# Routed experts of a two-layer decoder: the gated product turned by DRAM and VectorE instead of TensorE

## The chip, the cores and the metric

One core of one Trainium2 chip runs the whole program. The time is the device time of one execution in microseconds; the kernel before takes 2071.18 us (median of three runs, 2070.22 to 2071.78). A profile is one execution recorded by the hardware profiler; line numbers such as L1244 are lines of the kernel before.

TensorE (PE) multiplies, and a row PEld is its loading of weights; VectorE is DVE in the profile, ScalarE is ACT, GpSimd is POOL and SyncE is SP. SP, ACT and POOL can issue DMAs. A DMA issued by SP or ACT goes to a hardware queue (q1 in the profile is SP's, q10 is ACT's), one issued by POOL to the software queue q0.

## The reference

Two decoder layers work on x of 16 blocks x 128 tokens x 512, each with self-attention, cross-attention and a feed-forward part, a layer norm after each of the six parts. Only the last part, the mixture of experts, is touched by the change:

```python
logits = x @ gate_weight.T                      # E = 8 experts
topk_w, topk_idx = top_k(softmax(logits), 2)    # combine[t, e] = weight of a chosen expert, else 0
gu  = einsum('th,efh->tef', x, gate_up_weights) # F = 352, gate and up
act = silu(gu[..., :F]) * gu[..., F:]
y   = einsum('tef,te,ehf->th', act, combine, down_weights)
sgu = x @ shared_gate_up.T                      # a shared expert, Fs = 704
y   = y + (silu(sgu[:, :Fs]) * sgu[:, Fs:]) @ shared_down.T
x   = layernorm(x + y)
```

All values are float32.

## The kernel before

Five stages come first: first attention, second attention, the ternary feed-forward part, and the two attentions of the second layer. They are the same in both kernels. The last stage computes the router, sorts each (token, choice) pair into a slot of its expert, and writes the token's row into `slots_x` in DRAM, with its weight and its destination in two columns ahead of it (`told`). Each expert's slots are padded to whole tiles of 128 rows, so there are NT = 39 tiles at most. Meanwhile PE computes the shared expert's hidden values (`hidden`, L1116), and keeps its down products (`po`, L1299 and L1307) as small tasks that are dealt out between the tiles.

The loop over the 39 tiles is a pipeline of steps. A `Tile` has these parts:

- `load` (L1214): POOL gathers the expert's weights, `ew`, 128 rows of 4352 floats, by an indirect DMA. Three buffers are held. Where a buffer already holds the right expert, the index is out of bounds and nothing is moved.
- `fetch` (L1226, L1228): SP loads the tile's rows from `slots_x` in four parts of 64 KB (`xs`), in an order in which VectorE's transpose of 32 x 32 squares completes the turn of the whole tile, and `told`.
- `turn` (L1233): that transpose on VectorE, 128 x 512, from `xs` to `xsT`.
- `up` (L1244): on PE the gate product `rg` and the up product `ru`, four matmuls each (a float32 matmul is two passes in the profile, so eight rows each); Silu on ScalarE (L1249); the product `ract` on VectorE (L1251).
- `turn_act` (L1256 to L1259): three PE transposes of `ract` against the identity into PSUM (`rt`), and two VectorE copies into `ractT`.
- `down` (L1265): three matmuls into `ry`. When they are done POOL may issue the weights of the tile after the next but one (`following.load()`, the same buffer). VectorE scales the result by the routing weight (L1276), and POOL adds it into `sums` in DRAM by an indirect DMA (L1277).

In step s the code calls `turn_act` of tile s-2, `turn` of s, `up` of s-1, `down` of s-2, and then deals one share of `po`. A planner orders the instructions of each engine, except those under `keep_in_program_order`, which stay as written. The order on PE after the first tiles is: `rt` of tile t-1, `rg` and `ru` of t, `ry` of t-1, some `po`; so `ry` of a tile stands behind `rg` and `ru` of the next tile.

The same kind of turn by way of DRAM is used elsewhere in the kernel: in the second stage `sq` is stored to `away` (L628) and read back in four loads as `pT` (L631), and `Turn` (L145, L151) does it for x.

Of the kernel before, what the change touches and what calls it, by code (L numbers as in the profile page):

```python
# [12 lines left out]
F32 = mybir.dt.float32  # L13
F32R = mybir.dt.float32r
AF = mybir.ActivationFunctionType
ALU = mybir.AluOpType
AX = mybir.AxisListType

P = 128
# [14 lines left out]
FE = 352  # L34
NX = E + 2
FS = 2 * FE
ECH = (128, 128, 96)
# [3 lines left out]
NT = 2 * NB + E - 1  # L41
# [5 lines left out]
def decoder_kernel(ctx: ExitStack, tc: tile.TileContext, a: dict, out: bass.AP):  # L47
    nc = tc.nc
# [4 lines left out]
    dram = ctx.enter_context(tc.tile_pool(name="dram", bufs=1, space=bass.MemoryType.DRAM))  # L53
# [19 lines left out]
    def bank(tag, shape, name):  # L73
        return psum.pool.tile(shape, F32, tag=tag, name=name, bufs=psum.banks[tag])
# [4 lines left out]
    ident = const.tile([P, P], F32, tag="ident", name="ident")  # L79
# [52 lines left out]
    QP = P // 4  # L132
# [206 lines left out]
    with tc.tile_pool(name="p1", bufs=1) as p1:  # L339
# [10 lines left out]
        with tc.tile_pool(name="p1a", bufs=1, side="right") as p1a:  # L350
# [5 lines left out]
            w = p1a.tile([P, KC, 640], F32, tag="w", name="w")  # L356
# [340 lines left out]
    with tc.tile_pool(name="p3", bufs=1) as p3:  # L697
# [34 lines left out]
        for g in range(NG):  # L732
# [4 lines left out]
            for f in range(NF0):  # L737
# [4 lines left out]
                for dst, wt in ((pa, w1), (pb, w2)):  # L742
                    for k in range(KC):
                        for n in range(2):
                            nc.tensor.matmul(  # L745
                                dst, lhsT=wt[:, k, f * P : (f + 1) * P], rhs=xs[n][:, k, :],
                                start=(k == 0 and n == 0), stop=(k == KC - 1 and n == 1),
                            )
                sg = p3.tile([P, TG], F32, tag="sg", name="sg", bufs=2)
# [11 lines left out]
            else:  # L761

                for n in range(2):
                    t = pre.tile([P, 2, 3 * D], F32, tag="pre", name=f"wq4{n}")
# [168 lines left out]
    QP = P // 4  # L933
# [93 lines left out]
    with tc.tile_pool(name="p6", bufs=1, reuse_waits="tile") as p6:  # L1027
        acts, halves = {}, {}
# [8 lines left out]
        def gate_up(w):  # L1037
            return w[:, 0:GU].rearrange("p (k f) -> p k f", k=KC)
# [10 lines left out]
        with tc.tile_pool(name="p6a", bufs=1, side="right", reuse_waits="tile") as p6a:  # L1049
# [14 lines left out]
            tr = bank("mm", [P, GB, P], "tr")  # L1064
# [7 lines left out]
            def gt(name, shape=(P, NB, E)):  # L1072
                return p6a.tile(list(shape), F32, tag=name, name=name)


            lg, sc, top, eq = (gt(n) for n in ("lg", "gsc", "top", "eq"))
            m = gt("gm", (P, NB))
# [123 lines left out]
        with tc.tile_pool(name="p6r", bufs=1, side="right", reuse_waits="tile") as p6r:  # L1201
# [3 lines left out]
            class Tile:  # L1205
# [32 lines left out]
                def up(self):  # L1238
                    gu = gate_up(self.w)
                    pg = bank("sc", [P, FE], "rg")  # L1240
                    pu = bank("sc", [P, FE], "ru")
                    for dst, off in ((pg, 0), (pu, FE)):
                        for k in range(KC):
                            nc.tensor.matmul(  # L1244
                                dst, lhsT=self.xT[:, k, :], rhs=gu[:, k, off : off + FE],
                                start=(k == 0), stop=(k == KC - 1),
                            )
                    sg = p6.tile([P, FE], F32, tag="sg", name="rsg", bufs=3)
                    nc.scalar.activation(sg, pg, AF.Silu)  # L1249
                    self.act = p6r.tile([P, FE], F32, tag="ract", name="ract", bufs=2)  # L1250
                    nc.vector.tensor_tensor(self.act, sg, pu, ALU.mult)  # L1251

                def turn_act(self):
                    tr = bank("pt", [P, 3, P], "rt")
                    for m_, mw in enumerate(ECH):
                        nc.tensor.transpose(tr[:mw, m_, :], self.act[:, m_ * P : m_ * P + mw], ident)  # L1256
                    self.actT = p6r.tile([P, 3, P], F32, tag="ractT", name="ractT", bufs=2)
                    nc.vector.tensor_copy(self.actT[:, 0:2, :], tr[:, 0:2, :])
                    nc.vector.tensor_copy(self.actT[: ECH[2], 2, :], tr[: ECH[2], 2, :])  # L1259

                def down(self, following):
                    dn = down_w(self.w)
# [56 lines left out]
            ahead = {}  # L1319
# [15 lines left out]
            for step in range(NT + 2):  # L1335
                if 3 <= step + 2 < NT:
                    ahead[step + 2] = Tile(step + 2)
                    ahead[step + 2].fetch()
                if 0 <= step - 2:
                    ahead[step - 2].turn_act()  # L1340
                if step < NT:
                    ahead[step].turn()
                if 0 <= step - 1 < NT:
                    ahead[step - 1].up()
                if 0 <= step - 2:
                    ahead.pop(step - 2).down(ahead[step + 1] if step + 1 < NT else None)
                if step < NT:
                    share.deal()
# [188 lines left out]
```

## Time and profile before

| what | value |
|---|---|
| median of the runs | 2071.18 us |
| profiled execution, its own time | 2073.39 us |
| its span, first to last instruction | 2071.6 us |
| PE busy in the span | 2014.1 us, 97% |
| VectorE, ScalarE, POOL busy | 878.6, 627.6, 646.8 us |
| routed-expert tiles, first `rg` to about the last `ry` | 1667 to 2021 us |
| of these 354 us: PE, VectorE, ScalarE, POOL busy | 343.6, 104.6, 18.1, 97.5 us |
| DMA engines busy in these 354 us | 69% (software queue 57.0%, SP's queue 11.7%) |
| mean granted TensorE clock | 0.992 of full speed |

A row of groups gives the line, the engine, the operation, what is written from what, the shape and the count; then the busy time and the mean length of one in ns; then the idle time of the engine just before, and what ended it. A row of the timeline gives start and length in us, then the same names, and in brackets the idle time before. A row of a DMA queue gives packets, MB, and the time of its packets as a share of 16 engines over the window. Releasers are inferred from semaphore events, and the lengths of matmuls overlap.

### The profile page before, as it was taken

What the parts mean: (1) busy time and instruction counts of PE and PEld (TensorE: products, weight loads), DVE (VectorE), ACT (ScalarE), POOL (GpSimd) and SP (SyncE); (2) the same over time, 40 slices, a digit from 0 to 9 for tenths busy, and PEclk for the clock granted to TensorE, in tenths of its full rate; (3) what the DMA queues carried; (4) which work ended last, traced back from release to release, by engine and by line L of the source; (5) the groups of instructions that cost most, each with busy time, mean ns of one, the idle gap of its engine ahead of it and who ended that gap; (6) DMA issues with size and microseconds to landing.
All of it is one profiled execution on the core that took longest, in us unless ns stands there. A gap on an engine that the chain in (4) does not pass through costs nothing.

```text
span 2071.6 us, 25330 instructions
## 1 busy us (share of the span) xinstructions
PE 2014.1 (97%) x9093; PEld 1115.7 (54%) x9093; DVE 878.6 (42%) x1763; ACT 627.6 (30%) x2107; POOL 646.8 (31%) x674
## 2 busy tenths in 40 slices
PE   8999999999999999999999999999899999999997
PEld 4555554444444458888554445555544455555552
DVE  4777732444554254432134314777731122232234
ACT  3555532333333333222310112766622200000002
POOL 6445530111211113233322113455613222223223
PEclk9999989999999999999999999999999999999999
DMA  9201231344432232001310018500023256786844
GB/s 249 78 25 40 104 124 52 104 127 137 132 117 83 66 118 71 21 11 54 143 51 22 11 34 266 204 22 21 27 66 118 87 141 178 226 237 188 247 108 168
DMA packets 155470, 221.58 MB, mean 107 GB/s; under 512 B 49616, under 2 KB 110416, under 8 KB 150608
## 3 DMA queue, kind: packets, MB, share of 16 engines
q1 hardware_dynamic: 140448, 146.51, 22.6%
q0 software_dynamic: 13792, 72.14, 11.6%
q8 instruction: 72, 1.18, 0.2%
q10 hardware_dynamic: 1104, 1.31, 0.2%
q14 instruction: 54, 0.44, 0.1%
HBM read 182.73 MB, written 72.69 MB: 123 GB/s over the span
## 4 chain that ended last, share of the span: by engine, by line
PE 85%; DMA 5%; DVE 4%; POOL 3%; ACT 2%; issue 1%; SPq 0%; POOLq 0%; DVEq 0%; ACTq 0%
PE po L649 10%; PE po L176 7%; PE pq L590 5%; PE pq L841 5%; PE pq L165 5%; PE pg L1116 4%; PE ry L1265 4%; PE po L772 4%; PE pa L745 4%; PE pb L745 4%; DMA ew<-in_l1f_w_dram,which 4%; PE rg L1244 4%; PE ru L1244 4%; PE pu L1116 3%; PE pv L851 3%; PE av L637 3%
## 5 line engine op out<-in xcount | busy, mean ns | idle before, releaser
L226 POOL TENSOR_TENSOR p<-p,rs 128x512 f32<-128x512 f32 x192 | 200.0, 1043 | 504.0 <-DVE rs L225 494.7
L649 PE MATMUL po<-mT,cc 128*128 128x512 f32 x512 | 231.5, 600 | 0.2 <-ACT cc L642 0.2
L219 ACT ACTIVATE p<-t,nmx 128x128 f32<-128x128 f32 x512 | 198.6, 390 | 34.0 <-POOL p L226 10.2
L649 PEld LDWEIGHTS po<-mT,cc 128*128 128x128 f32 x512 | 95.1, 190 | 114.3 <-issue 106.3
L219 ACT ACTIVATE p<-sc,nmx 128x128 f32<-128x128 f32 x256 | 90.2, 374 | 117.8 <-DVE nmx L214 110.4
L590 PE MATMUL pq<-xT,wqr 128*128 128x512 f32 x256 | 115.7, 593 | 2.9 <-ACT xT L129 2.9
L1214 POOL DMA_INDIRECT ew<-in_l1f_w_dram,which x39 | 40.6, 1042 | 249.1 <-PE ry L1265 182.8
L176 PE MATMUL po<-wo,oT 128*128 128x512 f32 x256 | 116.9, 600 | 0.4 <-ACT qkT L454 0.4
L1249 ACT ACTIVATE rsg<-rg 128x352 f32<-128x352 f32 x39 | 18.1, 464 | 326.4 <-PE rg L1244 310.1
L115 POOL TENSOR_SCALAR ve<-mv 128x1 f32<-128x1 f32 x80 | 18.1, 226 | 303.0 <-DVE mv L113 289.1
L1244 PE MATMUL rg<-ew,xsT 128*128 128x352 f32 x312 | 101.8, 469 | 10.4 <-DMA ew<-in_l1f_w_dram,which 9.6
L841 PE MATMUL pq<-xT,wq 128*128 128x512 f32 x256 | 110.6, 592 | 0.7 <-ACT xT L129 0.7
L1265 PE MATMUL ry<-ew,ractT 128*128 128x512 f32 (+1 forms) x234 | 106.9, 592 | 0.0
L122 POOL TENSOR_SCALAR x<-x,mv,rstd 128x512 f32<-128x512 f32 x48 | 100.5, 2094 | 4.5
L1244 PE MATMUL ru<-ew,xsT 128*128 128x352 f32 x312 | 98.7, 459 | 0.0
L219 ACT ACTIVATION_READ_ACCUMULATOR p<-t,nmx 128x1 f32 x512 | 96.1, 188 | 0.0
L233 DVE COPY pT<-pt 128x512 f32<-128x512 f32 x128 | 86.6, 679 | 19.4 <-PE pt L231 19.4
L756 POOL TENSOR_TENSOR hl<-ht,hh 128x512 fp32r<-128x512 f32 x44 | 57.4, 1306 | 108.2 <-ACT hh L754 108.2
L231 PEld LDWEIGHTS pt<-ident,p 128*128 128x128 f32 x512 | 60.0, 141 | 55.7 <-issue 41.5
L1116 PE MATMUL pg<-xT,sw_gu 128*128 128x512 f32 x192 | 86.5, 593 | 0.0
L1277 POOL DMA_INDIRECT sums<-ry,place x39 | 61.8, 1585 | 74.7 <-DMA sums<-ry,place 37.8
L1251 DVE TENSOR_TENSOR ract<-rsg,ru 128x352 f32<-128x352 f32 x39 | 20.3, 521 | 151.0 <-issue 140.4
(243 smaller groups left out, 3676.4 us busy)
## 6 DMA issues: line engine op xcount, KB each, us to landing
piece<-in_l0f_w_dram SPq DMA_DIRECT2D x48, 352.0 KB
away<-sq SPq DMA_DIRECT2D x32, 512.0 KB
pT<-away SPq DMA_DIRECT2D x128, 128.0 KB
raw<-in_l0x_raw_dram SPq DMA_DIRECT2D x8, 1728.0 KB
slots_x<-zero SPq DMA_DIRECT2D x1, 10023.0 KB
sums<-zero SPq DMA_DIRECT2D x1, 9984.0 KB
xs<-slots_x SPq DMA_DIRECT2D x156, 64.0 KB
x<-turned SPq DMA_DIRECT2D x128, 64.0 KB
```

The lines of the kernel that those rows point to most:

```text
L122: engine.tensor_scalar(x[b], x[b], mean, rstd, ALU.subtract, ALU.mult)
L165: nc.tensor.matmul(got["p"], lhsT=lhsT, rhs=rhs, start=(n == 0), stop=(n == len(pairs) - 1))
L176: nc.tensor.matmul(po, lhsT=oT[:, c, :], rhs=wo[:, c, :], start=(c == 0), stop=(c == KC - 1))
L219: nc.scalar.activation(self.p[:, j, :], src[:, j, :], AF.Exp, bias=nmx[:, j : j + 1], accum_out=self.sm[:, j : j + 1])
L226: nc.gpsimd.tensor_tensor(self.p, self.p, spread(rs, P), ALU.mult)
L590: nc.tensor.matmul(pq, lhsT=wqr[:, k, cols], rhs=xT[:, k, :], start=(k == 0), stop=(k == KC - 1))
L649: nc.tensor.matmul(self.po, lhsT=self.cc[:, 4 * par + j, :], rhs=mT[h], start=(par == 0 and j == 0), stop=(par == 1 and j == 3),)
L745: nc.tensor.matmul(dst, lhsT=wt[:, k, f * P : (f + 1) * P], rhs=xs[n][:, k, :], start=(k == 0 and n == 0), stop=(k == KC - 1 and n == 1),)
L841: nc.tensor.matmul(pq, lhsT=wq4[k // 2][:, k % 2, c * P : (c + 1) * P], rhs=xT[:, k, :], start=(k == 0), stop=(k == KC - 1))
L1116: nc.tensor.matmul(dst, lhsT=sw_gu[:, k, at : at + P], rhs=xTs[g][:, k, :], start=(k == 0), stop=(k == KC - 1),)
L1244: nc.tensor.matmul(dst, lhsT=self.xT[:, k, :], rhs=gu[:, k, off : off + FE], start=(k == 0), stop=(k == KC - 1),)
L1265: nc.tensor.matmul(po, lhsT=self.actT[:mw, m_, :], rhs=dn[:mw, m_, :], start=(m_ == 0), stop=(m_ == 2))
```

## The change

The gated product no longer goes through PE to be turned. The multiply on VectorE is split in two and writes `act` with its columns in the order (fourth, chunk, 32) instead of (chunk, fourth, 32). ScalarE's queue stores it to `acts` in DRAM (three buffers), and four loads, two on ScalarE's queue and two on SP's, bring it back with each fourth of the columns on its own 32 partitions. Each load waits for the store. Two VectorE transposes of 32 x 32 squares then write `ractT`. The up product's PSUM bank and the Silu tile are widened to 384 columns so that they can be viewed in fourths. In a step, `turn` of tile s is called ahead of `turn_act` of tile s-2. `down` is the same, and so is all other code.

```diff
                 def up(self):
...
-                    sg = p6.tile([P, FE], F32, tag="sg", name="rsg", bufs=3)
-                    nc.scalar.activation(sg, pg, AF.Silu)
-                    self.act = p6r.tile([P, FE], F32, tag="ract", name="ract", bufs=2)
-                    nc.vector.tensor_tensor(self.act, sg, pu, ALU.mult)
+                    sg = p6.tile([P, 3 * P], F32, tag="sg", name="rsg", bufs=3)
+                    nc.scalar.activation(sg[:, 0:FE], pg, AF.Silu)
+                    act = p6r.tile([P, FE], F32, tag="ract", name="ract", bufs=2)
+                    def fourths(t):
+                        return t.rearrange("p (m q a) -> p m q a", m=3, a=QP)
+                    for q, to in (
+                        (slice(0, 3), act[:, 0 : 9 * QP].rearrange("p (q m a) -> p m q a", q=3, m=3)),
+                        (slice(3, 4), act[:, 9 * QP :].rearrange("p (m q a) -> p m q a", m=2, q=1)),
+                    ):
+                        n = to.shape[1]
+                        tc.keep_in_program_order(nc.vector.tensor_tensor(
+                            to, fourths(sg)[:, 0:n, q], fourths(pu)[:, 0:n, q], ALU.mult
+                        ))
+                    self.away = dram.tile([P, FE], F32, tag="acts", name="acts", bufs=3)
+                    nc.scalar.dma_start(self.away, act)
+                    self.act = p6r.tile([P, 4, 3 * QP], F32, tag="ract4", name="ract4", bufs=2)
+                    for q in range(4):
+                        w = (3 if q < 3 else 2) * QP
+                        (nc.scalar, nc.sync)[q % 2].dma_start(
+                            self.act[q * QP : (q + 1) * QP, :, 0:w],
+                            self.away.rearrange("(t r) f -> r t f", r=QP)[:, :, 3 * q * QP : 3 * q * QP + w],
+                        )
 
                 def turn_act(self):
-                    tr = bank("pt", [P, 3, P], "rt")
-                    for m_, mw in enumerate(ECH):
-                        nc.tensor.transpose(tr[:mw, m_, :], self.act[:, m_ * P : m_ * P + mw], ident)
                     self.actT = p6r.tile([P, 3, P], F32, tag="ractT", name="ractT", bufs=2)
-                    nc.vector.tensor_copy(self.actT[:, 0:2, :], tr[:, 0:2, :])
-                    nc.vector.tensor_copy(self.actT[: ECH[2], 2, :], tr[: ECH[2], 2, :])
+                    to = self.actT.rearrange("p m (t r) -> p t m r", r=QP)
+                    act = self.act.rearrange("p t (m a) -> p t m a", a=QP)
+                    for rows, ms in ((P, slice(0, 2)), (ECH[2], slice(2, 3))):
+                        tc.keep_in_program_order(nc.vector.transpose(to[:rows, :, ms], act[:rows, :, ms]))
...
+                if step < NT:
+                    ahead[step].turn()
                 if 0 <= step - 2:
                     ahead[step - 2].turn_act()
-                if step < NT:
-                    ahead[step].turn()
```

## The prediction

> **What bounds the kernel now.** I read the busy shares first, then the groups of the routed-expert stage, then its order in time, and last the DMA queues in short windows. The page's first part has TensorE (PE) busy for 97% of the 2071.6 us span. The changed code runs from the first `rg` matmul to the last `ry`, about 1667 to 2021 us. Groups of that stage (busy us, mean ns of one | idle before):
>
> ```profile
> L1265 PE MATMUL ry<-ew,ractT 128*128 128x512 f32 (+1 forms) x234 | 106.9, 592 | 0.0
> L1244 PE MATMUL rg<-ew,xsT 128*128 128x352 f32 x312 | 101.8, 469 | 10.4 <-DMA ew<-in_l1f_w_dram,which 9.6 <-issue 0.8
> L1244 PE MATMUL ru<-ew,xsT 128*128 128x352 f32 x312 | 98.7, 459 | 0.0
> L1256 PE MATMUL rt<-ident,ract 128*128 128x128 f32 (+1 forms) x117 | 19.3, 274 | 0.0
> ```
>
> The means overstate PE, since matmuls overlap; starts in time do not. Here is one step (start, length in us):
>
> ```profile
> 1748.65 0.52 DVE L1251 TENSOR_TENSOR ract<-rsg,ru 128x352 f32<-128x352 f32 x1 [2.85 <-issue]
> 1751.40 1.03 POOL L1214 DMA_INDIRECT ew<-in_l1f_w_dram,which  x1 [5.92 <-PE ry L1265]
> 1751.83 0.49 PE L1256 MATMUL rt<-ident,ract 128*128 128x128 f32 x3
> 1751.95 0.34 SPq L1228 DMA_DIRECT2D told<-slots_x  x1
> 1752.16 2.53 PE L1244 MATMUL rg<-ew,xsT 128*128 128x352 f32 x8
> 1753.62 2.13 SPq L1226 DMA_DIRECT2D xs<-slots_x  x4
> 1756.89 2.74 PE L1265 MATMUL ry<-ew,ractT 128*128 128x512 f32 x6
> 1757.15 0.52 DVE L1251 TENSOR_TENSOR ract<-rsg,ru 128x352 f32<-128x352 f32 x1 [3.56 <-issue]
> 1759.90 1.04 POOL L1214 DMA_INDIRECT ew<-in_l1f_w_dram,which  x1 [5.57 <-PE ry L1265]
> ```
>
> A step is 8.50 us (1748.65 to 1757.15): rg and ru 4.73, ry 2.58, about two shared `po` passes 0.86, transposes 0.33 (1751.83 to 1752.16). The chain that ended last leaves PE in this stage for one thing only, the weights:
>
> ```profile
> 1759.90 11.73 DMA ew<-in_l1f_w_dram,which
> 1771.67 2.63 PE rg L1244 x8
> ```
>
> A gather really moves weights only when the slot's expert changes. The software queue's bytes per step show it: after the first tiles there are seven runs of three consecutive real gathers (2.2 to 2.7 MB in each such step, 0.3 MB in the others). Their waits cost PE 12.9 us: the weight-load row (PEld `rg`) shows that sum in 11 waits, and the 9.6 of the matmul row are the same waits seen again.
>
> The last view decides this case: the queues while a weight gather flies (1753.4 to 1758.6 us; packets, MB, share of 16 engines). SP's four `xs` loads were issued at 1753.62.
>
> ```profile
> q0 software_dynamic: 101, 1.76, 84.4%
> q1 hardware_dynamic: 18, 0.01, 0.7%
> ```
>
> In 5.2 us the hardware queue moved 18 packets. In 1673 to 1675 us, just behind another gather, it moved 862:
>
> ```profile
> q1 hardware_dynamic: 862, 0.39, 97.4%
> ```
>
> So loads on SP's queue nearly stand still until the gather is through, and an `xs` issued at 1753.6 drains by about 1762. Nobody notices today: `xs` is fetched two steps ahead.
>
> **The change part by part.**
>
> *Transposes leave PE.* 39 tiles x 0.33 us = 12.9 us, the whole possible gain. In a step ended by a weight wait it is worth nothing, since the gather's landing doesn't move.
>
> *VectorE.* The multiply becomes two, of 288 and 64 columns. The 352-column row takes 521 ns and the 512-column copy from PSUM 687, so about 1 ns a column over a fixed 160: 0.45 + 0.22, about 0.65 us together, 0.15 more. Two PSUM copies (0.42 + 0.28) become two square transposes; 512 columns take 697 ns (`xsT`), so 256 and 96 rows of 128 take about 0.43 + 0.30. Even. VectorE is busy 105 of 354 us here: hidden, except on the way of `act` below. `turn` now stands ahead of `turn_act`, so `xsT` isn't held up by it. Queued behind a late `turn_act` on VectorE are the next tile's multiply, `place` and the scaling of `ry`.
>
> *DMA issues.* Per tile one store and two loads on ScalarE's queue, two loads on SP's ahead of later `xs` and `told`. A store takes 0.34 us to issue and a load 0.43 (SP rows of the `away`/`pT` pair in the second stage). ScalarE is busy 18 of 354 us, so 1.2 us a tile are free; but its next Silu stands behind the two loads, which wait for the store. SP gains 0.86 to its 2.1 us of a step: hidden. That ScalarE has a queue of its own helps no further by the Trainium skill (same page as below, section "Issuing engines are not separate DMA queues"): all queues end in the same 16 engines and only issue time is saved; no trace here shows the two queues under load yet, so the new traffic is costed as if on SP's.
>
> *DMA time.* Sixteen 64 KB loads used 20.2% of 18 us of all engines (1104 to 1122 us), 0.91 us for four of 512 packets. The new four have 512 smaller packets: 0.6 (by bytes) to 0.9 (by packets). The store at the rate of the final 256 KB `sum` loads (0.75 us each) is 0.5. Together 1.1 to 1.4 us a tile; without the cover of the idle DMA (31% of the stage) it would delay gathers by just that.
>
> *The round trip, on the path.* Let m be the start of the multiply. Store issued at m+0.65; a dependent load after a 256 KB store could start 2.08 us after its issue (1017.97 to 1020.05), here about 1.9; second load of each queue 0.45 later; its landing about 2.1 (the 256 KB `sum` took 2.62). Landed m+5.1, turned m+5.8. `ry` needs it at 1756.89 less the 0.33: m+7.9. So 2.1 us of slack, covered by ry, po, rg and ru of other tiles, if the queues are free.
>
> They are not free in the runs. A gather is issued at m+2.75 and its packets run from 1.2 to 8.1 us after issue (2.3 to 7.7 for the second of a run, which first waits for the gather and scatter ahead of it).
> - First gather: the loads' packets start about 1 us after issue, m+3.5 to m+4.3, against its m+3.95. `told`, issued 0.55 us after the gather, still got through by 1753.4. I take no stall.
> - Second gather: this tile's store goes out at m+0.65 into the first gather, which lasts until m+2.7; it drains by m+3.9 and is confirmed at m+4.3. The loads' packets would start at m+5.3 to m+6.2, the second gather at m+5.05. `xs`, at 0.9 us behind a gather's start, was stopped. So the late ones wait until m+10.45; 0.8 to drain, 0.4 to confirm, 0.7 to turn: `ry` at m+12.5, a stall of 4.6 us.
> - Third gather: after that stall the multiply again starts just ahead of `ry`, with the queue free: no stall, but a gather lands 9.9 us after issue (1751.40 to 1761.30) and PE comes for it after about 9.3, later by some of the new traffic: 1.0 us.
>
> Here the Trainium skill speaks for the change ("DMA: Bandwidth & Descriptors", section "Queues, rings and completion order"): an engine takes turns between the queue rows it has work for, a packet at a time, and a packet holds some 9 to 17 descriptors. One of these DMAs is 8 rows per engine, one turn, so three turns behind gather packets of about 0.7 us add 2.1 us, just the slack: no stall, and 2071.2 - 12.9 + 2 = 2060. The row shows 18 packets in 5.2 us. I take the row.
>
> *Ends.* First tile: its SP loads stand behind up to eleven `xs` loads: 1.5 us. Last tile: the trip is bare, `ry` 1.5 us late, but the last scatter (2021.44) waits for the one before it: 0.5.
>
> *Sum.* 7 x (4.6 + 1.0) = 39.2; less 12.9 of waits absorbed, less 12.9 of transposes, plus 2.0: +15.4. With half of the 1.1 to 1.4 us of new traffic once per run on the gathers' chain (some 2 us, hence rounded up): +17. The profiled execution took 2073.39 us with a span of 2071.6; the difference of 1.8 stays, and the median of the runs shown (2071.18) is 2.2 below it, so I add to the median: 2088.
>
> **The rivals.**
> - *All three gathers of a run stop the loads.* For it: the margin at the first is 0.3 us, and `told` packets hold 8 bytes. Against: after a stall the queue is free. 21 stalls of 4.8 = 101; -25.8 + 2: about 2148.
> - *No load is stopped, but the traffic delays gathers.* For it: at the second gather the margin is only 0.25 us for the first pair. Then gathers bound the runs as today, later by 1.25 us twice per run (17), and -12.9 + 2, less where gaps take it: about 2075.
> - *Faster.* No load is stopped and the new traffic fits into the gaps between gathers. PE keeps its 0.33 where no gather ends the step, about 22 of 39: -7, +2: 2066. It decides once the second tile's store is confirmed about a microsecond earlier, at m+3.3, so that all loads precede the second gather. The DMA's idle 31% speaks for it, the back-to-back gathers against.
> - The transposes do go: the order of PE's instructions has none left, with `ry` of one tile still behind `rg`, `ru` of the next.
>
> **How the numbers follow.** Second gather alone stalls: 0.48, 2088, own range 2079 to 2105. All stall: 0.17. Traffic only: 0.22. Faster: 0.13. A measurement here tells about 0.2% (4 us) from no change. Faster 0.13; same 0.07 (a third of the traffic case); slower 0.80. Below 2064 I leave 0.06, above 2135 (partial stalls at the other gathers) about 0.10.
>
> **What would show it.** No `rt` on PE; `ry` waiting for VectorE's turned `act` in about seven steps, 4 to 5 us each, in the second step of each run; few `ew` waits left; steps without gathers at 8.17 us; the hardware queues stalled while gathers fly. Wrong if `ry` waits in every step (a trip longer than 7.9 us with free queues), if all gathers stall it, or if PE waits only for `ew`.

## The result, and the profile after

The changed kernel takes 2151.49 us (median of four runs, 2144.40 to 2152.52) beside 2070.70 us for the kernel before (2068.75 to 2071.78): a ratio of 1.0386, 95% interval 1.0367 to 1.0404. It is slower by 80 us, where the forecast was slower by 17 and its range ended at 2135.

The profiled execution took 2152.52 us with a span of 2150.7. Up to 1667 us the two traces agree; the whole difference lies between the first `rg` and the last `ry`, 431.5 us after (1666.0 to 2097.5) and 351.8 before (1667.5 to 2019.3). In the changed kernel `up` stays at L1244, the store is L1265, the loads L1269, the square transposes L1279, `ry` L1285.

The groups of that stage, from the page of the changed kernel (busy us, mean ns | idle before):

```profile
L1285 PE MATMUL ry<-ew,ractT 128*128 128x512 f32 (+1 forms) x234 | 128.1, 690 | 61.5 <-DVE ractT L1279 61.5
L1244 PE MATMUL rg<-ew,xsT 128*128 128x352 f32 x312 | 99.8, 463 | 14.4 <-DMA ew<-in_l1f_w_dram,which 14.3
L1285 PEld LDWEIGHTS ry<-ew,ractT 128*128 128x128 f32 (+1 forms) x234 | 49.9, 220 | 122.9 <-DVE ractT L1279 70.4
L1244 PE MATMUL ru<-ew,xsT 128*128 128x352 f32 x312 | 98.8, 459 | 0.0
```

`rt` is gone from PE, `rg` and `ru` are as long as before. Two things are new in the rows of `ry`: it waits 70.4 us for VectorE's turned product (nothing before), and its 234 rows themselves take 128.1 us instead of 106.9. The 14.3 us for the weights have not gone either.

The waits in 1660 to 2105 us (total, times, longest):

```profile
DVE ractT L1279 <- DMA ract<-acts: 162.5, 29, 12.2
PEld ry L1285 <- DVE ractT L1279: 70.4, 16, 9.0
```

Of the sixteen waits of `ry` ten are 4.0 to 9.0 us long and make 63 us; the other six are 0.9 to 1.6 us. VectorE in turn waits for the loads.

One late trip, the chain of work in order of time (start, length):

```profile
1704.04 0.59 DVE ract L1261 x2
1704.62 0.03 DVE place L1293
1704.65 6.99 DMA acts<-ract
1711.64 0.03 ACTq L1269
...
1712.08 8.18 DMA ract<-acts
...
1720.34 0.46 DVE ractT L1279
1720.80 0.04 issue
1720.84 5.03 PE ry L1285 x6
```

The store takes 7.0 us until its loads may start, and the last of these 8.2 us to land; in a trip without a gather beside it the loads are issued 1.9 us after the store, and VectorE begins to turn what they brought 4.65 us after the store's issue. The queues in 1704 to 1708, 1708 to 1711, 1712 to 1715 and 1716 to 1720 us show why (q0 is POOL's queue; packets, MB, share of 16 engines):

```profile
q0 software_dynamic: 78, 1.36, 94.8%
q1 hardware_dynamic: 54, 0.03, 2.2%
...
q0 software_dynamic: 173, 0.54, 70.3%
q1 hardware_dynamic: 610, 0.22, 31.1%
q10 hardware_dynamic: 142, 0.18, 16.3%
...
q0 software_dynamic: 72, 1.25, 99.1%
...
q1 hardware_dynamic: 798, 0.32, 41.6%
q0 software_dynamic: 159, 0.31, 39.4%
q10 hardware_dynamic: 263, 0.09, 8.6%
```

In the first window a weight gather flies, and of the store (on q10, issued at 1704.65) not one packet moves. In the second the store drains, side by side with the scatter of an earlier tile, whose small packets follow the gather on q0. In the third the next gather flies: the loads were issued at 1711.7, and not one packet of a hardware queue moves in 3 us. Where nothing is in the way, the first packet on q10 follows 0.85 us behind a store's issue and about 1.1 us behind a load's, in this trace; here the store's took 4.15 us and the load's 3.49. In the fourth the loads share the engines with the next scatter and with four `xs` loads issued at 1712.5.

How long `ry` itself takes, from the timeline, ahead of this trip and behind it:

```profile
1704.64 2.74 PE L1285 MATMUL ry<-ew,ractT 128*128 128x512 f32 x6
...
1720.84 5.03 PE L1285 MATMUL ry<-ew,ractT 128*128 128x512 f32 x6 [5.87 <-DVE ractT L1279]
```

The same six rows take nearly twice as long after the wait. The windows (length; then busy us of PE, PEld, VectorE, ScalarE, POOL; granted clock; DMA share; GB/s) show the clock, after and then before:

```profile
1667.00:2021.00 354.00, 287.84 (x777) 150.84 (x776) 84.61 (x226) 14.86 (x32) 80.84 (x62) 0.92 0.70 199
```

```profile
1667.00:2021.00 354.00, 343.62 (x1076) 191.77 (x1075) 104.61 (x242) 18.10 (x39) 97.53 (x74) 1.00 0.69 194
```

The same view in short windows around this wait: PE stands idle in one, and the clock is at half in the two that follow.

```profile
1715.03:1718.44 3.41, 0.00 (x0) 0.00 (x0) 0.00 (x0) 0.00 (x0) 0.00 (x0) 1.00 1.05 257
1718.45:1721.86 3.41, 1.02 (x2) 0.50 (x3) 1.17 (x5) 0.00 (x0) 0.00 (x0) 0.50 0.30 57
1721.86:1725.27 3.41, 3.41 (x5) 1.35 (x4) 0.00 (x0) 0.00 (x0) 0.00 (x0) 0.50 0.38 100
1725.28:1728.69 3.41, 3.41 (x10) 1.54 (x9) 2.48 (x5) 0.00 (x0) 2.24 (x2) 1.00 0.40 82
```

So by the trace: 70.4 us of waits, 21.2 of slower `ry`, 4.7 more waiting for weights (14.3 for 9.6 in the matmul row), less 12.9 of transposes: 83 us, beside 79.7 by which the stage grew.

### The profile page after: what moved, and what is told of

Read it like the earlier page. It is cut to its first block, busy times and chain, and to the rows that moved or that the text cites. A ratio compares the mean times of both kernels' runs of the same rounds, so it can differ in the third digit from the quotient of the medians.

```text
span 2150.7 us, 25471 instructions
## 1 busy us (share of the span) xinstructions
PE 2025.2 (94%) x8976; PEld 1109.4 (52%) x8976; DVE 879.7 (41%) x1802; ACT 627.2 (29%) x2107; POOL 646.7 (30%) x674
## 4 chain that ended last, share of the span: by engine, by line
PE 78%; DMA 10%; DVE 5%; POOL 3%; issue 2%; ACT 2%; SPq 0%; ACTq 0%; DVEq 0%; POOLq 0%
PE po L649 9%; PE po L176 7%; PE pq L590 5%; PE pq L841 5%; PE pq L165 5%; DMA ract<-acts 4%; PE ry L1285 4%; PE pg L1116 4%; PE po L772 4%; PE pa L745 4%; PE pb L745 4%; PE pu L1116 3%; DMA xs<-slots_x 3%; PE pv L851 3%; PE av L637 2%
## 5 line engine op out<-in xcount | busy, mean ns | idle before, releaser
L219 ACT ACTIVATE p<-t,nmx 128x128 f32<-128x128 f32 x512 | 198.6, 390 | 34.0 <-POOL p L226 10.2
L1285 PE MATMUL ry<-ew,ractT 128*128 128x512 f32 (+1 forms) x234 | 128.1, 690 | 61.5 <-DVE ractT L1279 61.5
L1244 PE MATMUL rg<-ew,xsT 128*128 128x352 f32 x312 | 99.8, 463 | 14.4 <-DMA ew<-in_l1f_w_dram,which 14.3
L1285 PEld LDWEIGHTS ry<-ew,ractT 128*128 128x128 f32 (+1 forms) x234 | 49.9, 220 | 122.9 <-DVE ractT L1279 70.4
L1244 PE MATMUL ru<-ew,xsT 128*128 128x352 f32 x312 | 98.8, 459 | 0.0
L1279 DVE STREAM_TRANSPOSE ractT<-ract 128x256 f32<-128x256 f32 x78 | 24.4, 350 | 162.5 <-DMA ract<-acts 162.5
L1244 PEld LDWEIGHTS rg<-ew,xsT 128*128 128x128 f32 x312 | 58.0, 189 | 61.8 <-issue 30.7
```

The lines of the kernel that those rows point to most:

```text
L219: nc.scalar.activation(self.p[:, j, :], src[:, j, :], AF.Exp, bias=nmx[:, j : j + 1], accum_out=self.sm[:, j : j + 1])
L1244: nc.tensor.matmul(dst, lhsT=self.xT[:, k, :], rhs=gu[:, k, off : off + FE], start=(k == 0), stop=(k == KC - 1),)
L1285: nc.tensor.matmul(po, lhsT=self.actT[:mw, m_, :], rhs=dn[:mw, m_, :], start=(m_ == 0), stop=(m_ == 2))
```

## The experiments

The theory at this point: a store or load that meets a gather is stopped, `ry` waits, and the wait also costs clock. Rivals: the trip is too long by itself; the new packets take their time from the gathers; ScalarE's queue stalls; something else in the change costs. All times are medians beside runs of the kernel before on the same chip (2068.4 to 2071.5 us). Where two kernels are compared, their ratios are subtracted and 0.01 is counted as 20.7 us.

| run | us | ratio to before, 95% |
|---|---|---|
| nogather_before | 2058.58 | 0.9940 (0.9922 to 0.9958) |
| nogather_after | 2052.82 | 0.9915 (0.9898 to 0.9933) |
| notrip | 2069.24 | 1.0001 (0.9991 to 1.0011) |
| traffic | 2081.41 | 1.0067 (1.0047 to 1.0087) |
| sp_after | 2173.08 | 1.0505 (1.0473 to 1.0537) |
| split4_before | 2054.30 | 0.9931 (0.9909 to 0.9953) |
| split4_after | 2119.83 | 1.0234 (1.0212 to 1.0256) |
| noscatter_before | 2062.12 | 0.9961 (0.9949 to 0.9974) |
| noscatter_after | 2120.45 | 1.0239 (1.0213 to 1.0265) |
| direct16 | 2217.54 | 1.0716 (1.0698 to 1.0734) |
| direct16_split4 | 2182.17 | 1.0542 (1.0524 to 1.0559) |
| apart_before | 2056.06 | 0.9931 (0.9915 to 0.9948) |
| loose_after | 2089.58 | 1.0091 (1.0074 to 1.0109) |
| warm_after | 2142.49 | 1.0345 (1.0324 to 1.0366) |
| stall9 | 2056.77 | 0.9936 (0.9919 to 0.9953) |
| stall16 | 2056.84 | 0.9935 (0.9918 to 0.9951) |
| copies13 | 2071.68 | 1.0003 (0.9995 to 1.0012) |
| copies27 | 2136.35 | 1.0312 (1.0294 to 1.0330) |

### Both kernels without repeated gathers

```diff
-            nc.vector.tensor_tensor(again[:, HELD:], expert[:, HELD:], expert[:, : NT - HELD], ALU.is_equal)
+            nc.vector.memset(again[:, HELD:], 1.0)
```

> The kernel before, but no tile after the first three moves weights (every later index is out of bounds, so the gathers are issued and move nothing; the products use old weights). Every theory: only the 12.9 us of weight waits go, about 2058 us. This is the base for the next run.

> The changed kernel with the same edit: no weights moved after the first three tiles. Theory A (the trip of the product through DRAM is stopped by weight gathers in flight): no ry waits any more but at the first and last tile, and the missing transposes show, 5 to 13 us below the kernel before with the same edit, about 2045 to 2053. Theory B (the trip is too long by itself, whatever flies beside it): still 50 us or more above it, about 2110 or more.

With only the first three tiles' weights fetched, the changed kernel is the faster one, by 5.8 us. Its only wait of `ry` is at the first tile:

```profile
PEld ry L1285 <- DVE ractT L1279: 2.0, 1, 2.0
```

VectorE begins to turn the product 4.4 to 5.6 us after the store's issue in every later tile but one (7.7), and most steps take 8.17 us for 8.50. So the trip is not too long by itself; gathers make it so. Of the 12.9 us of transposes the ends take back 7: the first `ry` starts 4.6 us later (1681.76 for 1677.15), and the last stands 7.73 us behind the one before it instead of 4.63, a part of which is `po` work that the planner moved ahead of it.

### The squares without the trip, and the trip's packets without anyone waiting

```diff
-                    self.away = dram.tile([P, FE], F32, tag="acts", name="acts", bufs=3)
...
+                    self.prod = act
...
-                        tc.keep_in_program_order(nc.vector.transpose(to[:rows, :, ms], act[:rows, :, ms]))
+                    tc.keep_in_program_order(nc.vector.transpose(
+                        self.actT[:, 0:2, :], self.prod[:, 0 : 2 * P].rearrange("p (m a) -> p m a", m=2)
+                    ))
...
```

The second kernel keeps the store and the loads and only has the squares read `self.prod`.

> The changed kernel without the store and the four loads: VectorE squares the product straight from where the multiply wrote it, so the blocks land in other places than in the reference; PE's work and VectorE's are those of the changed kernel. If the trip through DRAM is the whole of the loss, this ends between 2058 (2070.7 less the 12.9 of transposes) and 2065 us (the 5.8 us that the pair without weight gathers showed as the gain). If something else in the change costs (VectorE's two multiplies, the order of turn and turn_act), it stays above 2075 us.

> As the kernel without the trip, but the store and the four loads are issued as in the changed kernel and nothing waits for what the loads bring (the products come from misplaced blocks as there). If the loss is the wait of ry for the trip, this ends within 5 us of the kernel without the trip, about 2058 to 2070 us. If the loss is what the new packets take from the weight gathers, it stays near the changed kernel, above 2110 us. Where the multiply of the tile after next has to wait for a late store, a part of the loss could come back: a few us.

`notrip` gains nothing, which neither expectation had: with the gathers in place the transposes' 12.9 us are worth about 0. Its PE waits for the weights instead (15.0 us, 9.6 before):

```profile
L1244 PE MATMUL rg<-ew,xsT 128*128 128x352 f32 x312 | 100.4, 465 | 15.8 <-DMA ew<-in_l1f_w_dram,which 15.0 <-issue 0.8
```

The packets by themselves cost 0.0066, about 14 us; the limit of 5 us was passed, but most of the loss isn't there. 7.2 us of it are a wait that the changed kernel's own trace doesn't have: `ru` for a PSUM bank that Silu has yet to read, while ScalarE's queue holds two loads ahead of the next Silu.

```profile
L1244 PE MATMUL ru<-ew,xsT 128*128 128x352 f32 x312 | 100.4, 465 | 7.3 <-ACT rsg L1249 7.2
```

What remains, 1.0386 less 1.0067, about 66 us, is the price of `ry` depending on the trip.

### All five DMAs on SP's queue

```diff
-                    nc.scalar.dma_start(self.away, act)
+                    nc.sync.dma_start(self.away, act)
...
-                        (nc.scalar, nc.sync)[q % 2].dma_start(
+                        nc.sync.dma_start(
```

> The changed kernel with the store and all four loads on SP's queue. If the loads stand behind the gather's packets in the 16 shared engines, the queue that issues them doesn't matter: within 15 us of 2151 us. If ScalarE's queue (a load that waits for the store ahead of the next Silu) is what stalls, it falls to 2130 us or below; if SP's xs loads behind the waiting store come late, it rises above 2170 us.

ScalarE's queue is not the cause: without it the kernel loses another 25 us (0.0119). The waits of `ry` are 77.8 us in 22, for 70.4 in sixteen, and the rows of `rg` take 106.3 us for 99.8, so most of the extra lies outside these waits. On SP's queue the store now waits 17.3 us for loads of an earlier trip. That `xs` behind a waiting store makes the rest, as the expectation has it, was not tested.

### Gathers of quarter rows, in both kernels

```diff
-                    tc.keep_in_program_order(nc.gpsimd.indirect_dma_start(
-                        out=self.w, out_offset=None, in_=table,
+                    for j in range(4):
+                        tc.keep_in_program_order(nc.gpsimd.indirect_dma_start(
+                            out=self.w[:, j * (EW // 4) : (j + 1) * (EW // 4)], out_offset=None, in_=table,
...
```

> The changed kernel, with each weight gather cut into four gathers of a quarter of the columns, so that a packet is 4.3 KB and not 17 KB. Theory A, with turns taken packet by packet: the trip's packets get four times as many turns beside a gather, waits of ry fall from 70 us to 20 us or less, about 2075 to 2100. If it is not the size of the packets that stops the hardware queues, but any gather in flight: within 10 us of 2151. POOL issues 117 more gathers of about 1 us each, in its idle time.

> The kernel before with each weight gather issued as four of a quarter row each (4.2 KB instead of 17 KB), as in the run of the changed kernel that was cut so (2119.8 us). Control for that run. If the smaller rows help only the trip, this ends at 2065 to 2080 us (four issues on POOL instead of one, the gather's end little moved), and the loss of the changed kernel shrinks from 81 us to some 45. If smaller rows make every gather faster or slower by itself, it moves by more than 10 us from 2070.7 us and the run of the cut changed kernel has to be read against that.

Cutting 17 KB rows to 4.4 KB makes the kernel before faster by 14 us: its waits for weights are gone, and the stage is 336.5 us long, as without gathers. The change then still costs 0.0303, about 63 us instead of 80. Long packets are therefore about a fifth of the loss. The waits of `ry` did not fall to 20 us or less as the turns by packet would have it; they are 67.7 us, in 22. The queues in 1767.8 to 1769.8 us of the changed kernel with quarter rows, its loads having been issued at 1766.6:

```profile
q0 software_dynamic: 167, 0.64, 95.5%
q1 hardware_dynamic: 1, 0.00, 0.1%
```

The gather moves 167 packets, and the hardware queues one. The stops are shorter, though: the first packet of a late load comes up to 3.4 us behind its issue here, and up to 4.6 us in the changed kernel.

### Without the scatters, in both kernels

```diff
-                    nc.gpsimd.indirect_dma_start(
-                        out=sums, out_offset=bass.IndirectOffsetOnAxis(ap=place, axis=0),
-                        in_=y, in_offset=None, compute_op=ALU.add,
-                    )
```

> The changed kernel without the 39 scatters that add ry to the sums (the output lacks the routed experts' part). Theory: behind each gather the scatter's packets hold the same 16 engines for another 2 to 3 us, which makes a stop 6 to 9 us long and adds stops. Then the loss against the kernel before without scatters falls from 81 to between 25 and 50 us (seven stalls of about 4.6 us with their slower matmuls). If the gathers alone stop the trip, the loss stays within 15 us of 81.

> The kernel before without the scatters: the control for the other. The second gather of a run no longer waits behind a scatter on POOL's queue, so a part of the 12.9 us of weight waits goes: 2058 to 2071 us.

The loss falls from 80 to 58 us (0.0278): further than the 15 us that the gathers alone would allow, not as far as the 25 to 50 us of the theory. The waits of `ry` go from sixteen to ten, and none is longer than 7.4 us:

```profile
PEld ry L1285 <- DVE ractT L1279: 48.1, 10, 7.4
```

So the scatters are about 22 of the 80 us, and the gathers hold the larger part. How much of the 22 is the scatters' own packets, and how much the next gather that stands behind them on POOL's queue, was not separated.

### Half the trip

```diff
-                    self.away = dram.tile([P, FE], F32, tag="acts", name="acts", bufs=3)
-                    nc.scalar.dma_start(self.away, act)
...
+                        for t in range(4):
+                            (nc.scalar, nc.sync)[t % 2].dma_start(
+                                self.act[q * QP : (q + 1) * QP, t, 0:w],
+                                act[t * QP : (t + 1) * QP, 3 * q * QP : 3 * q * QP + w],
+                            )
```

> The changed kernel with the trip cut to half: no store to DRAM, sixteen copies a tile (32 rows of 384 bytes each) from the product to the turned layout within SBUF, eight on ScalarE's queue and eight on SP's. If it is the second step that loses (loads that may start only once the store is confirmed, and then meet the next gather), the stalls of ry go and the time falls to that of the traffic alone, 2070 to 2090 us. If any packet of a hardware queue that meets a gather or a scatter is stopped, whichever step it belongs to, stalls remain in the runs of gathers: above 2110 us.

> The same half trip, with each weight gather issued as four of a quarter row each. The kernel before with gathers cut so takes 2054 us. If the half trip is hidden, this ends at 2050 to 2065 us and is the fastest of the kernels with the change; if the copies still meet gathers and scatters, it stays above 2090 us.

Both are slower than the changed kernel. `ry` waits 133.5 us in 25 waits. But the test is not clean: eight copies take 5.2 us to issue on each queue where four loads took 1.7 us on both together, and beside gathers the issue stretches further (ScalarE's queue, the first tile and one that met two gathers):

```profile
1675.29 5.22 ACTq L1268 DMA_DIRECT2D ract<-ract  x8
...
1728.84 13.26 ACTq L1268 DMA_DIRECT2D ract<-ract  x8
```

The issue stretches because the copies wait for one another: in the trace they report their landing on eight semaphores used in turn, and a later copy is issued when an earlier one has landed (the third one of the long row at 1733.61, after a landing at 1733.59). On SP's queue:

```profile
SPq L1268 <- DMA ract<-ract: 49.9, 24, 5.0
```

The run shows that leaving out the store doesn't help if the number of DMAs grows; whether a half trip with few DMAs would be hidden stays open.

### A step more for the trip, and its control

The weights are gathered in two parts, from two arrays, gate and up as soon as their last products are done; in the changed kernel the down weights get a fourth buffer, two other tiles (`ractT` and `row`) lose buffers to make room for it, and `ry` runs a step later.

```diff
+                    if later is not None:
+                        later.gather(0)
...
-                        following.load()
+                        following.gather(1)
...
-                if 0 <= step - 2:
-                    ahead[step - 2].turn_act()
+                if 0 <= step - 3:
+                    ahead[step - 3].turn_act()
```

(The last pair of lines is in `loose_after` alone.)

> The kernel before, transposes on TensorE, with the weights gathered in two parts in the same way (three slots for both): gate and up of a tile right after the products that last use the slot, some 3 us ahead of the single gather. Control for the kernel with a step more. The 12.9 us of weight waits go for the most part: 2055 to 2062 us. If the two halves, as two sets of smaller rows, are no earlier, it stays at 2070 us.

> The changed kernel with a step more for the trip: ry of a tile runs three steps behind its load instead of two, so the turned product has 16 us from its multiply instead of 7.9. To keep the weights long enough, they are gathered in two parts: gate and up into three slots, right after the products that last use the slot, down into four. If the loss is the trip meeting gathers and scatters (trips of up to 15.8 us), the stalls of ry all but go: 2045 to 2065 us, since the weights' own waits go as well. If the trip stretches with whatever slack it gets, because more of the DMA's time is spoken for, it stays above 2090 us.

The control comes out as expected, 14 us faster than before; no weight wait is left and its stage is 336.5 us as well. The changed kernel with a step more for the trip is back at 2089.6, a loss of 33 us against its control instead of 80. It is not hidden even so. Its waits of `ry`:

```profile
PEld ry L1301 <- DVE ractT L1295: 27.7, 10, 4.9
```

Six of the ten are 3.0 to 4.9 us; those trips were turned 14 to 18 us after the store's issue. The DMA engines are busy 87% of 1667 to 2021 us there (70% in the changed kernel): the same work in less time, and more down weights. The result lies between the two expectations. That the trip stretches with what the queues have to do fits it, but the other differences of this kernel were not taken apart.

### The clock

Six matmuls on resident weights ahead of `ry`, in the ten tiles that had waited:

```diff
+                    if self.t in (4, 10, 15, 18, 20, 23, 25, 28, 31, 32):
+                        warm = bank("pt", [P, D], "warm")
+                        for n in range(FILL):
+                            tc.keep_in_program_order(nc.tensor.matmul(
+                                warm, lhsT=sw_dn[:, 0, 0:P], rhs=sw_dn[:, 0, :], start=(n == 0), stop=(n == FILL - 1)
+                            ))
```

> The changed kernel, with six idle matmuls (128x512, result unused, 5.2 us) added ahead of the ry of the ten tiles whose turn came 4 us or more late in the profile. Theory A with a second term, that PE's clock falls while it waits and ry, po and rg then run at half speed: the added matmuls fill time that was lost anyway and hold the clock up, so adding work makes it faster by 20 to 27 us, about 2127, with a granted clock near 0.99. If the clock is no part of it: 2151, unchanged, or some us slower where a wait is shorter than the filler.

Fifty microseconds of added work make the kernel 9 us faster, less than half of what the clock theory gave.

```profile
L1292 PE MATMUL ry<-ew,ractT 128*128 128x512 f32 (+1 forms) x234 | 112.3, 617 | 23.5 <-DVE ractT L1280 23.5
L1288 PE MATMUL warm<-sw_dn 128*128 128x512 f32 x120 | 53.1, 592 | 0.0
```

`ry` falls from 128.1 to 112.3 us of 106.9 at full clock, and its waits from 70.4 to 31.9; the fillers take 53.1. But waits moved to tiles without fillers (8.0 and 7.5 us at tiles 16 and 29), so the run doesn't size the clock. Two more were to do that in a kernel without gathers, by idle work on VectorE ahead of the copy of `rt`:

```diff
+                    if self.t % 3 == 0 and 6 <= self.t <= 33:
+                        for _ in range(LATE):
+                            tc.keep_in_program_order(nc.vector.transpose(idle, idle))
```

> The kernel before without repeated weight gathers (2058.6 us; only the first three tiles' weights are fetched, so the products are not the reference's), and in ten tiles VectorE runs nine idle square transposes of 0.70 us before it copies the turned product out of PSUM. The copy has 3.9 us to spare ahead of ry (1752.98 to 1756.89 in the trace of before), so ry waits 9 x 0.70 - 3.9 = 2.4 us in each of the ten: 2083 us in either theory, since a wait of 2.5 us and less left ry at 2.84 us in the trace of the changed kernel.

> The same with sixteen idle transposes: ry waits 16 x 0.70 - 3.9 = 7.3 us in each of the ten tiles. If a wait costs its own length, 2058.6 + 73 = 2132 us. If TensorE's clock falls in a wait of that length and ry then takes 5.0 instead of 2.74 us, as behind the long waits of the changed kernel, 2.3 us more each: 2155 us, and the granted clock of the stage falls to about 0.93.

Neither tested anything: nothing tied the idle work to the product, the planner put it where VectorE was free, `ry` waited 1.2 us in all and both took 2056.8 us. The next pair repeats the copy itself, which has to follow `rt` and precede `ry`:

```diff
-                    nc.vector.tensor_copy(self.actT[:, 0:2, :], tr[:, 0:2, :])
+                    for _ in range(COPIES if self.t % 3 == 0 and 6 <= self.t <= 33 else 1):
+                        tc.keep_in_program_order(nc.vector.tensor_copy(self.actT[:, 0:2, :], tr[:, 0:2, :]))
```

> As the run with nine idle transposes, but what delays ry now hangs on the transposes' result: the kernel before without repeated weight gathers (2058.6 us), and in ten tiles VectorE copies the turned product out of PSUM thirteen times instead of once, 0.42 us each. The copies begin about 1752.4 on the clock of the step shown and take 5.5 us, with the next tile's multiply and place among them some 0.7 and a wait of 0.5 for it; ry is ready for them at 1756.9, so it waits about 2.2 us in each of the ten. Both theories say 2058.6 + 22 = 2081 us.

> The same with twenty-seven copies: ry waits about 2.2 + 14 x 0.42 = 8.1 us in each of the ten tiles. If a wait costs its own length, 2058.6 + 81 = 2140 us. If TensorE's clock falls in it and ry then takes 5.0 instead of 2.74 us, 2162 us.

Thirteen copies made waits of 0.2 to 1.1 us only, 3.5 in all; twenty-seven made six of 7.37 us, not ten. The totals alone therefore decide nothing, the two traces do. A wait with its `ry`, and the stage's group, with twenty-seven copies:

```profile
1938.23 0.50 PEld L1267 LDWEIGHTS ry<-ew,ractT 128*128 128x128 f32 x2 [7.37 <-DVE ractT L1260]
1938.23 5.49 PE L1267 MATMUL ry<-ew,ractT 128*128 128x512 f32 x6 [7.12 <-DVE ractT L1260]
...
L1267 PE MATMUL ry<-ew,ractT 128*128 128x512 f32 (+1 forms) x234 | 123.1, 667 | 43.6 <-DVE ractT L1260 43.6
```

With thirteen:

```profile
L1267 PE MATMUL ry<-ew,ractT 128*128 128x512 f32 (+1 forms) x234 | 107.2, 593 | 0.8 <-DVE ractT L1260 0.8
```

Between the two kernels `ry` waits 43 us more (46.3 for 3.5), its rows take 15.9 more, `rt` waits 4.1 more: 63 us, of 64.7 measured. No DMA of the trip is here, so the slower `ry` comes from the wait alone: one of 7.4 us costs about 10. In each of the six the granted clock is at half for 10.2 us (from 1933.5 to 1943.7 in the one shown). The clock theory holds; its share in the changed kernel is the 21.2 us read above, a reading of the trace that agrees in kind with these six waits and was not taken away by itself.

## Why the prediction was wrong

The sign and the mechanism were right: `ry` does wait for a trip stopped by the gathers. The size was not, and the changed kernel lies outside the range. The step that failed is the sum of stalls, "7 x (4.6 + 1.0)", with no stall at the first and third gather of a run and no term for the clock. The trace has 70.4 us of waits for the forecast's 32.2, and 21.2 us more in slower rows of `ry`. Sorted by the gather that the trip's loads met, the ten long waits are:

| gather of a run | forecast | measured waits, us |
|---|---|---|
| first | none | 9.0, 4.6, 4.0: 17.7 |
| second | 7 of 4.6: 32.2 | 6.4, 6.4, 8.0, 6.7, 5.8: 33.3 |
| third | no stall of `ry` | 6.3, 5.8: 12.0 |

- **The trip with free queues.** Foretold: loads 1.9 us behind the store, turned at m+5.8. Measured: loads 1.9 us behind the store, and the turn, which begins 4.65 us and ends 5.3 us behind it, over at about m+5.9. Right, as were the steps of 8.17 us and VectorE's even account (879.7 us busy in the span, 878.6 before).
- **First gather: no stall.** Right in four of the seven runs, where the loads were issued 1.9 us behind the store. In the other three they were issued 2.2 to 3.6 us behind it, and the margin of 0.3 us was gone. The longest wait of all is one of these:

```profile
1858.01 0.34 ACTq L1265 DMA_DIRECT2D acts<-ract  x1
...
1860.49 1.03 POOL L1214 DMA_INDIRECT ew<-in_l1f_w_dram,which  x1 [4.99 <-PE ry L1285]
...
1861.65 0.85 ACTq L1269 DMA_DIRECT2D ract<-acts  x2
...
1874.27 5.11 PE L1285 MATMUL ry<-ew,ractT 128*128 128x512 f32 x6 [8.46 <-DVE ractT L1279]
```

- **Second gather: 4.6 us in seven runs.** The trace has 33.3 us of such waits, as foretold, but by chance: five stalls, each longer. "It drains by m+3.9 and is confirmed at m+4.3" became m+7.6 on the chain shown above, since the store's first packet moved only at m+4.8, behind the gather ahead, and then beside a scatter. "0.8 to drain, 0.4 to confirm" became 5 us, from 1715.2 to 1720.3, since another scatter and the `xs` loads drained beside it. The prediction named the scatter only as something that the gather waits for, and gave it no DMA time; the runs without scatters put 22 us of the loss on them.
- **Third gather: no stall of `ry`.** Right in five runs. In the other two the first gather had stalled a trip, the second passed, and the next store met the second gather and its loads the third.
- **The clock.** No term of the sum at all. The Trainium skill has the rule ("TensorE: Matmul & The Clock Gate", "Part 1: The HAM clock gate"): the clock is halved by a monitor that watches a window of about 3.4 us, and a cold array needs about that time of work to be warm again. The trace agrees: all changes of the granted clock in this stage lie whole multiples of 3.41 us apart, and in nine of the ten long waits the clock fell to half. Those nine made the six rows 4.5 to 5.5 us long, for 2.84 behind the short waits and the tenth. Put on the seven waits of 4.6 us, with 2.2 us each, it would have added 15 us to the forecast; on the waits as they came it is 21.
- **Transposes, -12.9.** The work left PE, but was worth nothing beside gathers: `notrip` stands at 1.0001. The prediction said that a step ended by a weight wait gains nothing, and then took all 39 steps off; its own case "Faster" counts 22.
- **New traffic, about +2.** About 14 us by the run without the dependence. The Silu behind the loads was named, and costed at nothing.
- **Weight waits absorbed, 12.9 less, 7.0 back.** They are 14.3 us in the matmul row after, for 9.6 before: the stalls did not absorb them.
- **Row or rule.** The row taken against the rule on turns by packet was the right choice: with the rule the forecast would have been 2060. The quarter rows show that shorter packets shorten the stops but don't restore the turns.

The rival in which all three gathers of a run stall gave 2148 us, close to the measured time, but by 21 waits of 4.8 us; the trace has ten, most of them longer, and a slower `ry`. It was right that a gather of any of the three places can stop a trip; its total is near by chance.

## What to carry to other kernels

A round trip through DRAM that fits its slack with free queues must be costed beside everything that POOL's queue will have in flight in that slack, scatters as well as gathers, and twice, since the loads can start only when the store is confirmed. A margin of 0.3 us against a gather is none: it was lost here in three runs of seven. A long wait of TensorE is dearer than its length (7.4 cost about 10 us here), and work taken off TensorE is worth only what the next bound leaves: here nothing while the weights' gathers stood next in line. What did help was to have the weights sooner, by quarter rows or by two parts, with the transposes left where they were: 2054.3 and 2056.1 us, ratio 0.9931 for both, the fastest of the twenty kernels that compute the whole result.

## What the runs showed of the hardware beyond that

- While a gather flew, a hardware queue with work could move nothing at all: no packet from 1863 to 1866 us with loads issued at 1861.65, beside 17 KB rows (q0 moved 56 packets), and one in 2 us beside rows of 4.4 KB. By the Trainium skill ("DMA: Bandwidth & Descriptors", "Queues, rings and completion order") an engine alternates between the queues that have work, a packet at a time; in 1704 to 1708 us the records look so for SP's queue (54 packets beside 78), but not for ScalarE's, and not in 1712 to 1715 or 1863 to 1866. What decides between the two is open.
- Whether a wait halves the clock depends on where it falls among the windows of 3.41 us, and not on its length alone. In the changed kernel a wait of 3.5 us (the 4.0 of the table, in the matmul row) lay across two windows and left PE 1.61 and 1.73 us busy in them: the clock stayed. In the kernel before, a wait of 2.2 us for weights lay in one window and left 1.17 us: the next window ran at half clock. So a window need not be idle throughout for that. After (first two rows) and before:

```profile
2022.23:2025.64 3.41, 1.61 (x6) 0.73 (x4) 0.00 (x0) 0.00 (x0) 0.00 (x0) 1.00 1.03 388
2025.64:2029.05 3.41, 1.73 (x4) 0.87 (x5) 1.17 (x5) 0.00 (x0) 0.00 (x0) 1.00 0.97 253
...
1932.83:1936.24 3.41, 1.17 (x6) 0.46 (x4) 1.93 (x4) 0.00 (x0) 1.03 (x1) 1.00 1.08 250
1936.24:1939.65 3.41, 3.41 (x6) 2.06 (x7) 0.00 (x0) 0.00 (x0) 1.53 (x1) 0.50 0.99 416
```

- `ry` behind a long wait takes up to 5.49 us, twice its 2.74, so the whole of it can run at half clock; the mean granted clock of the stage shows this only as 0.92.
